# Scheduler priority for the ends, turned rows, routing and plan of a decoder's first expert layers

## The chip, the core and the metric

The kernel runs on one core of a Trainium2 chip. A core has five engines with instruction queues of their own: TensorE (PE in the profile, PEld for its weight loads), VectorE (DVE), ScalarE (ACT), GpSimd (POOL) and SyncE (SP), which here only starts DMA transfers. Each engine works through its queue in order; they wait for one another by semaphores. The metric is the device time of one execution in microseconds (us).

## What is computed

Two decoder layers over `x` of 16 batches of 128 rows by 256, everything in float32. Each sublayer's output is added to its input and normalised:

```
x = LN(x + causal attention, 16 heads of 64)            # layer 0
x = LN(x + sum_e gate_e * relu(x Win_e) Wout_e)         # 8 experts, gates from two inputs
x = LN(x + 2 shared experts + top-2 of 16 routed ones)
x = LN(x + banded attention, 16 heads of 16)            # layer 1
x = LN(x + cross attention on ctx)
x = LN(x + g/(g+1e-6) * sum_e (gelu(x w1_e + b1_e) w2_e + b2_e))   # 8 experts, all of them
```

The third line is the one that matters here. Router logits `x @ router_w` give a softmax; the best two of 16 experts and their weights are found for every row. The kernel collects the rows of each expert, so that each routed expert multiplies only its own rows.

## The kernel before, in words

**Groups and streams.** The 16 batches form 4 groups of 4 (512 rows). A piece of work is a Python generator that yields an estimated duration in us after each portion, or a condition, or a time until which it waits. A `Weaver` (lines 216 to 256) interleaves them while the program is written: a main stream (attention layers), a side stream `dense` (expert layers), and short streams, which are taken first whenever their time has come. `after` (1270) adds a short stream. `run` (1276) names the layers: (0, g) is attention, (1, g) the first expert layer of group g, (2, h) the routed experts of half h (groups 2h and 2h+1), (3, g) and (4, g) the attentions of layer 1, (5, g) the last experts. The dense stream does (1,0) (1,1) (2,0) (1,2) (1,3) (2,1) and then the four last expert layers; (2, h) is written only once the half's plan has been written (1279).

**From program order to queues.** The Tile framework makes the queue of each engine before launch. It steps through a simulated time: when an engine is free, it takes, of the instructions whose inputs are ready by its estimates, the one that ranks first, which is the one written first in the program. An instruction written later can go earlier if it is ready earlier. `tc.high_priority()` makes what is written inside it rank as if written at the program's start. Tiles with the same tag share a fixed number of buffers; they are handed out in the order in which the program asks. PSUM has two banks each of the tags H, M and O and one double bank S. Projections, hidden layers, turned rows, routing logits and the plan's counts all use H; expert products use M; attention uses S for scores and O for turned weights and products.

**The first expert layer** (`ensemble0`, 807, with `products`, 681). TensorE computes hidden layers (tag H) and, by a Strassen scheme, 7 block products per expert (tag M), which DVE adds up in `acc` (721). When the last expert is done, POOL and DVE combine the 7 sums into `y` (743 to 753), and `finish` adds a short stream: `products_end`, followed by `tail(1, g)`.

**`products_end`** (756) waits 2.5 us of written time. In two halves it turns `y` on TensorE (763), adds it to `x` and takes the statistics on DVE (290, 300, 301); `done` (303) computes the deviation's inverse on POOL (308) and normalises on DVE (310).

**`tail(1, g)`** (1243) waits, then `transposed` (261) turns the 4 normalised batches on TensorE (268); DVE copies the first turned half (270), ACT the second (272). `route` (840) follows: 8 matmuls for logits (845), and a chain of some 25 small DVE instructions and one on ACT (858 to 892) for the best two experts and their weights.

**`plan`** (928) follows the routing of the second group of a half. Two matmuls count the rows per expert (936), a chain of DVE instructions (942 to 987) computes where each row goes (`places`), and 16 indirect DMAs on POOL (992) scatter the rows of `x` to `copies` in HBM. `experts0` (1003) first does the two shared experts of both groups, then loads scattered rows (`load_rows`, 1063, which waits for all 16 scatters), turns them (`turn`, 1074) and does the 16 pairs of row tiles.

Of the kernel before, what the change touches and what calls it, by code (L numbers as in the profile page):

```python
# [29 lines left out]
def kernel(ctx: ExitStack, tc: tile.TileContext, a: dict, out: bass.AP):  # L30
# [15 lines left out]
    def bank(tag):  # L46
        return ps.tile([P, T], F32, tag=tag, name=f"ps{tag}")
# [7 lines left out]
    def transpose(out_, in_):  # L55
        n = in_.shape[0]
        return nc.tensor.transpose(out_, in_, ident[:n, :n])  # L57
# [36 lines left out]
    def load_up(name, *parts):  # L94
        return load_w("up", 1024, name, *parts, bufs=3)
# [114 lines left out]
    UNTIL = "until"  # L210

    class Stream:
        def __init__(self, gen):
            self.gen, self.at, self.can, self.share, self.over = gen, 0.0, None, 0.0, False

    class Weaver:

# [5 lines left out]
        def piece(self, t):  # L223

            t.can = None
            try:
                got = next(t.gen)
            except StopIteration:
                t.over = True
                return 0.0  # L230
            if callable(got):
                t.can = got
            elif isinstance(got, tuple):
                t.at = got[1]
            else:
                self.now += got
                return got
            return 0.0
# [19 lines left out]
    weaver = Weaver()  # L258


    def transposed(x, xT=None):

        if xT is None:
            xT = xp.tile([P, KC, T], F32, tag="xT", name="xT")
        for c in range(KC):
            pt = bank("H")
            for b in range(GB):
                transpose(pt[:, b * P:(b + 1) * P], x[:, b, c * P:(c + 1) * P])
            if c == 0:
                nc.vector.tensor_copy(xT[:, c, :], pt)  # L270
            else:
                last = nc.scalar.copy(xT[:, c, :], pt)
        return xT, last

    class Norm:
# [27 lines left out]
        def done(self, first=0, n=GB):  # L303
            at = slice(first, first + n)
            ve = sp.tile([P, GB], F32, tag="ve", name="ve")
            nc.vector.tensor_scalar(ve[:, at], self.mv[:, at, 1], EPS, None, ALU.add)  # L306
            rstd = sp.tile([P, GB], F32, tag="rstd", name="rstd")
            nc.gpsimd.tensor_tensor(rstd[:, at], ve[:, at], mhalf[:, at], ALU.pow)  # L308
            for b in range(first, first + n):
                nc.vector.tensor_scalar(  # L310
                    self.x[:, b, :], self.x[:, b, :],
                    self.mv[:, b, 0:1], rstd[:, b:b + 1], ALU.subtract, ALU.mult,
                )

    def project(pt, w, cols, xT):

        for c in range(KC):
            mm(pt, lhsT=w[:, c, cols], rhs=xT[:, c, :], start=c == 0, stop=c == KC - 1)
# [340 lines left out]
    def load_blocks(layer, e, g, w):  # L659

        if (layer, e) in in_hbm:
            got, = load_down("wb", in_hbm[layer, e])
            return got.rearrange("p s (q d) -> p s q d", q=2)

        raw, = load_w("up", 1024, "raw", w, bufs=3, later=True)
        raw = raw.rearrange("p (q l) (j d) -> p q l j d", l=2, j=2)
        b00, b01, b10, b11 = (raw[:, :, l, j, :] for l in range(2) for j in range(2))
        t = wp.tile([P, 7, 2 * P], F32, tag="down", name="wb0")
        blocks = t.rearrange("p s (q d) -> p s q d", q=2)
        minus = [(4, b01, b00), (5, b11, blocks[:, 4]), (2, blocks[:, 5], b10), (3, b11, b01)]  # L670
        for s, one, two in minus:
            step = nc.gpsimd.tensor_tensor(blocks[:, s], one, two, ALU.subtract)
            together(step, *transposed_by[g])
        for s, one in ((0, b00), (1, b10), (6, b11)):
            together(nc.gpsimd.tensor_copy(blocks[:, s], one), *transposed_by[g])
        held = dp.tile([P, 7, 2 * P], F32, tag=f"wb{layer}", name="wbd", bufs=8)
        nc.gpsimd.dma_start(out=held, in_=t)
        in_hbm[layer, e] = held
        return blocks
# [76 lines left out]
    def products_end(t, norm, scale, done):  # L756

        yield UNTIL, weaver.now + 2.5
        for i in (1, 0):
            pt = bank("H").rearrange("p (b d) -> p b d", b=2)  # L760
            for b in range(2):
                for j in range(2):
                    transpose(pt[:, b, j * P:(j + 1) * P], t[:, j, i, b * P:(b + 1) * P])
            for b in range(2):
                at = 2 * i + b
                norm.add(at, pt[:, b, :], None if scale is None else scale[:, at:at + 1])
            done(norm, 2 * i)
            yield 0.5
# [3 lines left out]
    def gates0(g):  # L772

        it = p2.tile([P, GB, P], I32, tag="it", name="it", bufs=1)
        nc.sync.dma_start(
            out=it, in_=a["itok_BxS2xS_0_7"][g * GB:(g + 1) * GB].rearrange("b k s -> k b s")
        )
        cx = load_ctx(g).rearrange("p b s -> p (b s)")
        held = dp.tile([8, T], F32, tag="gates", name="gatesd", bufs=NG)
        for q in range(2):  # L780
            chose = []
            for r in range(4):
                t = p4.tile([P, T], F32, tag="cw", name="chose")
                step = nc.vector.scalar_tensor_tensor(
                    out=t, in0=it.rearrange("p b s -> p (b s)"), scalar=float(4 * q + r), in1=cx,
                    op0=ALU.is_equal, op1=ALU.mult,
                )
                together(step, *transposed_by[g])
                chose.append(t)
            yield UNTIL, weaver.now + 3.5  # L790

            pg = bank("H")
            for r in range(4):
                mm(
                    pg[32 * r:32 * r + 32, :], lhsT=ones[:, :32], rhs=chose[r],
                    start=True, stop=True,
                )
            sums = p4.tile([P, T], F32, tag="cw", name="sums")
            nc.scalar.copy(sums, pg)
            for r in range(4):  # L800
                nc.sync.dma_start(
                    out=held[4 * q + r:4 * q + r + 1, :], in_=sums[32 * r:32 * r + 1, :]
                )
            yield 1.0
        gates_of[g] = held

    def ensemble0(x, xT, g):
        def load(e):
            gt = p2.tile([P, T], F32, tag="sg", name="gt")
            nc.sync.dma_start(out=gt, in_=gates_of[g][e:e + 1, :].to_broadcast([P, T]))  # L810
            return load_up(f"we0_{e}", a["L0_xattn_proj_in"][e])[0], gt

        def hidden(h, up, e, c):
            ph = bank("H")
            project(ph, up[0], slice(c * P, (c + 1) * P), xT)
            nc.vector.scalar_tensor_tensor(  # L816
                out=h, in0=ph, scalar=0.0, in1=up[1], op0=ALU.max, op1=ALU.mult
            )

        norm = Norm(x)  # L820
        yield from products(
            load, lambda e: load_blocks(0, e, g, a["L0_xattn_proj_out"][e]), hidden,
            lambda t: after(
                products_end(t, norm, None, lambda norm, b: norm.done(b, 2)), tail(1, g)
            ),
        )

# [175 lines left out]
    def experts0(half):  # L1003
# [153 lines left out]
        def collect():  # L1157
# [3 lines left out]
            for g in groups:  # L1161
# [15 lines left out]
                after(tail(2, g))  # L1177

        after(collect())

    def gate1(xT):
# [61 lines left out]
    def tail(number, g):  # L1243

        if number >= 0:
            yield UNTIL, weaver.now + 7.0
        xTs[g], last = transposed(xs[g], xTs[g])
        transposed_by[g] = [last]
        yield 0.9
        if number == 0:  # L1250
            yield from gates0(g)
        elif number in (1, 4):
            yield UNTIL, weaver.now + 2.5
            if number == 4:
                extra[g] = yield from gate1(xTs[g])
            else:
                yield from route(xTs[g], g)
                if written[g ^ 1] == 1:
                    yield from plan(g // 2)
        written[g] = number  # L1260
# [6 lines left out]
            out=out[at:at + 2].rearrange("b p d -> p b d"), in_=norm.x[:, b:b + 2, :]  # L1267
        )

    def after(*gens):  # L1270
        def both():
            for gen in gens:
                yield from gen
        weaver.short.append(Stream(both()))

    def run(number, g):

# [120 lines left out]
```

## Time and profile before

| | |
|---|---|
| median of 3 runs | 1773.87 us (1773.58 to 1775.16) |
| the profiled execution | 1788.15 us |
| its span, first to last instruction | 1786.5 us |
| TensorE granted clock, mean | 0.977 |
| TensorE busy | 1683.4 us, 94% |
| DVE, ACT, POOL busy | 1135.9, 658.8, 491.4 us |
| routing of groups 0 to 3, first DVE step (L858), first and last | 388.5 us, 1030.4 us |
| scatters of the first plan, of the second (L992), first start | 575.08 us, 1053.83 us |

In the profile a line such as L858 is a line of the kernel. A row of a timeline gives the start, the duration, engine, line, operation, output and inputs by the program's names, the shape and the count of merged instructions; in brackets stands how long the engine had been idle before it and what ended that wait. Matmuls of one group are listed as pairs of passes, since float32 takes two. A row of a stage gives its start and end, its length, then the busy time and number of instructions of PE, PEld, DVE, ACT and POOL, the granted TensorE clock (1.00 is full), the DMA share and GB/s. The "chain that ended last" follows the execution back from its last instruction: at each step to what released it.

### The profile page before, as it was taken

The numbers are of one execution on the slowest core, as the hardware profiler recorded it, in microseconds if no ns is written. First come the engines' busy times: TensorE is split into PE (matmuls) and PEld (weight loads), VectorE is DVE, ScalarE is ACT, GpSimd is POOL, SyncE is SP. The second block draws the span as 40 slices with busy tenths as digits, with TensorE's granted clock in tenths as the row PEclk, the third lists the DMA queues.
The fourth block names the chain that finished last, engine by engine and source line by source line (L and its number), as shares of the span: only waits on it lengthen the run. The fifth ranks groups of instructions, "written<-read, shape, count | busy, mean of one in ns | idle before, by whom it ended". The sixth has DMA issues, their size and how long they took to land.

```text
span 1786.5 us, 21794 instructions
## 1 busy us (share of the span) xinstructions
PE 1683.4 (94%) x7644; PEld 1043.0 (58%) x7644; DVE 1135.9 (64%) x2209; ACT 658.8 (37%) x1758; POOL 491.4 (28%) x492
## 2 busy tenths in 40 slices
PE   9999999999998899999999888979999999999996
PEld 6656556666665565555556455546555555556664
DVE  4565655576657336777886754685667766685544
ACT  4534311111124250034121434642955668373121
POOL 5311223210012304132321341473533133230000
PEclk9999999999999899999999988989999999999998
DMA  9321333433311396332313018533241211212331
GB/s 269 120 72 41 107 133 121 136 100 115 124 51 39 109 312 230 110 109 78 96 58 114 16 39 298 166 117 112 100 139 60 76 55 68 75 65 98 109 118 33
DMA packets 96702, 195.95 MB, mean 110 GB/s; under 512 B 15960, under 2 KB 58000, under 8 KB 96528
## 3 DMA queue, kind: packets, MB, share of 16 engines
q1 hardware_dynamic: 90688, 171.01, 28.8%
q0 software_dynamic: 5904, 23.54, 3.7%
q8 instruction: 61, 1.00, 0.3%
q14 instruction: 49, 0.40, 0.1%
HBM read 165.09 MB, written 37.81 MB: 114 GB/s over the span
## 4 chain that ended last, share of the span: by engine, by line
PE 71%; DVE 13%; issue 6%; ACT 5%; DMA 2%; POOL 2%; another core or an unknown queue 0%; POOLq 0%; DVEq 0%; ACTq 0%; SPq 0%
PE psH L52 40%; PE psM L52 19%; PE psO L57 3%; PE psS L52 3%; PE psO L52 3%; PE psH L57 2%; ACT e L369 2%; DVE nmax L354 1%; DVE x L310 1%; DMA wquad<-in_L_attn_W_Q 1%; DVE h L816 1%; DVE x L292 1%; POOL rstd L308 1%; DVE e L349 1%; DVE acc L721 1%
## 5 line engine op out<-in xcount | busy, mean ns | idle before, releaser
L52 PE MATMUL psH<-xT,we 128*128 128x512 f32 x1024 | 493.8, 604 | 8.3 <-ACT h L1226 4.9
L375 POOL TENSOR_TENSOR e<-e,inv 128x512 f32<-128x512 f32 (+1 forms) x128 | 190.3, 1487 | 501.2 <-DVE inv L374 446.5
L52 PEld LDWEIGHTS psH<-xT,we 128*128 128x128 f32 x1024 | 186.8, 191 | 173.9 <-issue 141.7
L369 ACT ACTIVATE e<-e,nmax 128x128 f32<-128x128 f32 x512 | 198.6, 389 | 196.6 <-DVE nmax L354 175.0
L52 PE MATMUL psM<-cm,wb 128*128 128x256 f32 x1024 | 265.1, 383 | 1.5 <-DVE acc L721 1.5
L52 PEld LDWEIGHTS psM<-cm,wb 128*128 128x128 f32 x1024 | 192.6, 191 | 70.6 <-issue 45.1
L721 DVE TENSOR_TENSOR acc<-psM,acc 128x512 f32<-128x512 f32 (+1 forms) x216 | 135.2, 626 | 123.5 <-PE psM L52 122.8
L52 PE MATMUL psM<-h,wb 128*128 128x256 f32 x768 | 200.7, 384 | 1.6 <-ACT h L1226 1.6
L384 ACT COPY eT<-psO 128x512 f32<-128x512 f32 x192 | 106.8, 584 | 232.9 <-PE psO L57 230.9
L52 PEld LDWEIGHTS psM<-h,wb 128*128 128x128 f32 x768 | 142.7, 190 | 65.1 <-issue 45.1
L1226 ACT ACTIVATE h<-psH,b 128x512 f32<-128x512 f32 x128 | 87.5, 688 | 188.5 <-PE psH L52 186.5
L816 DVE SCALAR_TENSOR_TENSOR h<-psH,gt 128x512 f32<-128x512 f32 x128 | 87.7, 686 | 80.9 <-PE psH L52 78.1
L57 PE MATMUL psO<-ident,e 128*128 128x128 f32 x768 | 118.3, 286 | 12.4 <-POOL e L375 8.5
L57 PEld LDWEIGHTS psO<-ident,e 128*128 128x128 f32 x768 | 90.7, 145 | 62.6 <-issue 37.7
L52 PE MATMUL psH<-xT,wquad 128*128 128x512 f32 x256 | 118.9, 608 | 3.4 <-DMA wquad<-in_L_attn_W_Q 3.1
L503 POOL TENSOR_TENSOR kb<-kT,hm 128x512 f32<-128x512 f32 x64 | 71.1, 1112 | 153.1 <-PE psS L52 99.1
L369 ACT ACTIVATION_READ_ACCUMULATOR e<-e,nmax 128x1 f32 x512 | 95.8, 187 | 0.0
L52 PE MATMUL psO<-eT,v 128*64 128x128 f32 (+1 forms) x1024 | 84.5, 346 | 6.2 <-ACT eT L384 5.4
L308 POOL TENSOR_TENSOR rstd<-ve,mhalf 128x4 f32<-128x4 f32 (+1 forms) x32 | 28.5, 890 | 211.8 <-DVE ve L306 211.7
L354 DVE TENSOR_REDUCE nmax<-e 128x4 f32<-128x512 f32 (+1 forms) x96 | 82.5, 859 | 1.9
L52 PE MATMUL psS<-kb,qT 64*128 64x512 f32 x256 | 74.2, 656 | 7.4 <-DVE e L349 3.0
L52 PEld LDWEIGHTS psH<-xT,wquad 128*128 128x128 f32 x256 | 47.2, 192 | 56.7 <-issue 47.4
(215 smaller groups left out, 2296.2 us busy)
## 6 DMA issues: line engine op xcount, KB each, us to landing
wb<-wbd SPq DMA_DIRECT2D x48, 896.0 KB
we<-in_L_xattn_proj_in SPq DMA_DIRECT2D x32, 512.0 KB
wt<-table SPq DMA_DIRECT2D x64, 256.0 KB
we<-in_L_ffn_w SPq DMA_DIRECT2D x32, 512.0 KB
wbd<-wb POOLq DMA_DIRECT2D x16, 896.0 KB
gt<-gatesd SPq DMA_DIRECT2D x32, 256.0 KB
results<-y SPq DMA_DIRECT2D x10, 768.0 KB
rows<-copies SPq DMA_DIRECT2D x6, 1024.0 KB
```

The source lines that it names most:

```text
L52: recent[0] = nc.tensor.matmul(*args, **how)
L57: return nc.tensor.transpose(out_, in_, ident[:n, :n])
L292: step = nc.vector.scalar_tensor_tensor(out=r, in0=y, scalar=scale, in1=r, op0=ALU.mult, op1=ALU.add)
L308: nc.gpsimd.tensor_tensor(rstd[:, at], ve[:, at], mhalf[:, at], ALU.pow)
L354: nc.vector.tensor_reduce(nmax.rearrange("p (s h) -> p s h", s=2), s, AX.X, ALU.max, negate=True)
L369: nc.scalar.activation(e[:, h, :], s[:, h // (n // 2), h % (n // 2), :], AF.Exp, bias=nmax[:, h:h + 1], accum_out=total[:, h:h + 1],)
L375: nc.gpsimd.tensor_tensor(e, e, inv.unsqueeze(2).to_broadcast([P, n, P]), ALU.mult)
L384: return eT, nc.scalar.copy(eT, pt)
L503: nc.gpsimd.tensor_tensor(kb, kT[:, c, at].unsqueeze(1).to_broadcast([P, 4, P]), hm4.unsqueeze(2).to_broadcast([P, 4, P]), ALU.mult,)
L721: nc.vector.tensor_tensor(to, pm[:, :len(slots), :], to, ALU.add)
L816: nc.vector.scalar_tensor_tensor(out=h, in0=ph, scalar=0.0, in1=up[1], op0=ALU.max, op1=ALU.mult)
L1226: nc.scalar.activation(h, ph, AF.Gelu, bias=b1[:, 4 * e + c:4 * e + c + 1])
```

## The change

A stream can carry a flag `early`. While a portion of such a stream is written, the program is inside `tc.high_priority()`. The short stream that follows each first expert layer, `products_end` and `tail(1, g)` with its routing and, for groups 1 and 3, the plan and its 16 scatters, is marked so. The other short streams, and the ends of the last expert layers (`store`), are not. What is computed, the instructions and the order in which the program writes them are the same.

```diff
     class Stream:
-        def __init__(self, gen):
+        def __init__(self, gen, early=False):
             self.gen, self.at, self.can, self.share, self.over = gen, 0.0, None, 0.0, False
+            self.early = early
...
             t.can = None
             try:
-                got = next(t.gen)
+                with tc.high_priority() if t.early else nullcontext():
+                    got = next(t.gen)
             except StopIteration:
...
             lambda t: after(
-                products_end(t, norm, None, lambda norm, b: norm.done(b, 2)), tail(1, g)
+                products_end(t, norm, None, lambda norm, b: norm.done(b, 2)), tail(1, g),
+                early=True,
             ),
...
-    def after(*gens):
+    def after(*gens, early=False):
         def both():
             for gen in gens:
                 yield from gen
-        weaver.short.append(Stream(both()))
+        weaver.short.append(Stream(both(), early))
```

## The prediction

> **What bounds the kernel now.** I read the page first, the utilisation by stage second, the chain of waits third, and the timeline around the two plans last. The page's first part:
>
> ```profile
> span 1786.5 us, 21794 instructions
> PE 1683.4 (94%) x7644; PEld 1043.0 (58%) x7644; DVE 1135.9 (64%) x2209; ACT 658.8 (37%) x1758; POOL 491.4 (28%) x492
> ```
>
> TensorE is busy 1683.4 of 1786.5 us, so 103 us of idle time are all that a new order can win, besides stretches at a reduced clock. The stages show where they lie (start and end in us, length, busy time of PE, PEld, DVE, ACT and POOL, granted clock, DMA share, GB/s):
>
> ```profile
> 380.00:400.00 20.00, 20.00 (x88) 13.18 (x87) 14.31 (x41) 3.65 (x12) 1.04 (x1) 1.00 0.29 92
> 575.00:604.00 29.00, 21.22 (x91) 13.40 (x91) 8.67 (x17) 5.11 (x19) 16.59 (x17) 0.80 0.42 145
> 950.00:1000.00 50.00, 49.37 (x191) 31.30 (x190) 33.49 (x65) 5.63 (x21) 7.04 (x7) 1.00 0.28 90
> 1003.00:1043.00 40.00, 28.92 (x133) 17.50 (x132) 30.70 (x71) 24.55 (x107) 18.86 (x15) 0.72 0.03 7
> 1071.00:1085.00 14.00, 6.20 (x31) 4.80 (x32) 3.14 (x10) 3.95 (x10) 2.27 (x3) 0.64 0.69 230
> ```
>
> Away from the plans TensorE is full (20.00 of 20, at clock 1.00, where group 0 is routed). Around a plan it is not: 7.8 us idle in 575 to 604, 11.1 in 1003 to 1043 at clock 0.72, 7.8 in 1071 to 1085 at 0.64. The second plan's path, from the timeline:
>
> ```profile
> 1022.77 1.09 PE L57 MATMUL psH<-ident,x 128*128 128x128 f32 x8
> 1024.58 0.64 DVE L270 COPY xT<-psH 128x512 f32<-128x512 f32 x1
> 1025.76 0.40 PE L52 MATMUL psH<-rw,xT 128*128 128x16 f32 x2
> 1026.61 0.56 ACT L272 COPY xT<-psH 128x512 f32<-128x512 f32 x1
> 1027.31 3.08 PE L52 MATMUL psH<-rw,xT 128*128 128x16 f32 x14
> 1030.43 0.23 DVE L858 TENSOR_REDUCE r_nm<-psH 128x4 f32<-128x64 f32 x1 [2.61 <-PE psH L52]
> ...
> 1053.83 1.07 POOL L992 DMA_INDIRECT copies<-x,r_places  x1 [3.81 <-DVE zT L541]
> 1072.92 0.96 POOL L992 DMA_INDIRECT copies<-x,r_places  x1 [0.30 <-issue]
> 1075.90 0.70 SPq L1068 DMA_DIRECT2D rows<-copies  x2
> 1078.39 0.90 PE L57 MATMUL psH<-ident,rows 128*128 128x128 f32 x3 [7.46 <-DMA rows<-copies]
> ```
>
> Turning, routing and planning take 1022.8 to 1053.5, the 16 scatters 1053.8 to 1073.9 back to back (0.96 plus 0.30 us each), and TensorE then waits 7.46 us for their rows. A microsecond saved on this path is one saved at 1078.39. The same path of the first plan runs from 537.5 to 575.08; there the rows are loaded at 597.10 but turned only at 626.95, behind the shared experts.
>
> **The change, part by part.** It removes and adds no instruction: 4 ends with their turned rows and routings, and 2 plans, keep all their work and only rank first when several instructions are ready for one engine. So I ask at each step which earlier-written instruction it now passes.
>
> DVE, routing and plan: nothing. In the first plan L354 (0.60 us) runs between L863 and L864, and L477 between L864 and L865. Those belong to attention units written later than the routing; they slip in while a step waits for its predecessor. Rank does not close such gaps. The 10.0 us of routing (1030.43 to 1040.45) and the 13.1 us from the plan's matmuls to its places (1053.53) stay, covered or not.
>
> POOL: the 32 scatters already run with no other POOL work among them (20.2 us for each 16, first to last end). SP issues nothing of the early pieces; its row loads wait for the scatters and move with them. Both are costed at the shift, no more.
>
> TensorE and PSUM: each early step takes its bank of tag H in turn, after the H tiles written before it, so it passes only work on banks S, O and M.
>
> First plan, three gains. The turn of the first y half, at 537.73, has its input from L751 at 536.23: up to 1.4 us, but the second half needs L753 (537.50), so I take half, 0.7. The turned x, ready at 546.19, is taken at 547.22 behind 8 records of values that began at 545.60: bound 1.0; the records already begun stay ahead, so 0.5. The routing matmuls start at 551.08 though the copy on ACT ends at 549.88, with transposes, an output and a product of attention between: bound 1.2, I take 1.1, since only a release is left. Sum 2.3, bounds 0 and 3.6. The attention passed here is late next; it has 7.8 us of idle TensorE after 575 to go into.
>
> Second plan. The turned x is done at 1023.86, but ACT copies it at 1026.61, after six exponentials begun from 1024.31 on, 0.385 us apart. Passing them brings the copy 2.3 us forward. TensorE cannot use it all: its scores run to 1025.83, and 16 routing records at this clock take 0.40 + 3.08 = 3.5 us, ending at 1029.3 instead of 1030.4. I take 1.2, between 0 and 2.4. Behind it come the passed exponentials, 0.56 us later each, and the four transposes of 1026.69; no dense work waits for them.
>
> The clock after that wait: it is granted at 0.64 on average from 1071 to 1085, so full speed returns late. If rows come 1.2 us earlier, some slow time may go. Were all the 6.20 busy us there at half speed, 3.1 would be slowness: the upper end; 0 is the lower. I take 0.6, a fifth of it, as the shift is a fifth of the 6.20. The Trainium skill, page "TensorE: Matmul & The Clock Gate", Part 1, speaks against counting on it: the gate looks at fixed windows of about 3.4 us, so an arrival inside the same window buys nothing. By that rule the term would be either 0 or a whole window's half, and this total 0.6 worse or 1.1 better; no row here fixes the window's phase after the shift.
>
> Second plan's sum 1.8, bounds 0 and 5.5.
>
> Losses, at the same steps in all four groups. In group 0 the second turn ends near 385.07, ACT's copy runs 385.10 to 385.69, and 1.89 us of products on bank M, 384.90 to 386.6, cover it before the routing matmuls. If these rank before the products, TensorE stands still for up to 0.7 us until the copy is there, in a stage where it has none to spare. The order is made beforehand by estimated times, so it would only happen where the estimate is early. I take two such places at 0.4, 0.8 us in all; the lower end is 0, the upper 20 places (two turns of y, two of x, one routing in each of 4 groups) at 0.7, 14 us. I stand near the lower end because the waits for turned x found now are small: nothing at group 0.
>
> Sum: 2.3 + 1.8 - 0.8 = 3.3 us less. The profiled execution took 1788.15 us (span 1786.5 and 1.65 around it) and would take 1784.85. The median of the three runs, 1773.87, lies 14.28 below it; I carry the difference over: **1770.6 us**. A change of 0.2%, about what a measurement of this kernel can tell from none, is 3.55 us; the forecast lies just inside it.
>
> **Rivals.**
>
> *Cover lost (slower).* Place: the twenty TensorE steps above, worst where it is full, at 380 to 400 and 950 to 1000. TensorE works in order, so a turn or routing matmul put before products that are ready makes those wait too, and DVE's sums and the next hidden layers behind them. Price 0.7 us each; the gains of 4.1 are eaten at six places, and 0.2% slower is reached at eleven. Twelve give 1773.87 - 4.1 + 8.4 = 1778.2. For it: before has waits of up to 2.8 us on DVE x L290 and 1.8 on r_one L876. Against: the order is made from estimated readiness, and the present one already lets the early steps through soon.
>
> *Nothing.* The early steps hold low places already, because the weaver prefers short streams; the bank order keeps the rest. Then 1773.9, give or take 1. For it: DVE and POOL show no overtaking at all. Against: ACT's 2.75 us from turn to copy at 1023.86.
>
> *More goes.* At 591.5 to 597.9 the chain has 6.39 us of "another core or an unknown queue": DVE L349 and, behind it, TensorE (7.78 us) stand until the first scatters have landed. If a changed order lets that work fall before the scatters' end, these go too: 3.3 + 6.4 = 9.7 less, 1764.2. Against: nothing in the change touches the scatters.
>
> **How the numbers follow.** Forecast 0.42 (own range 1766 to 1773, which reaches further down than up from 1770.6, so 0.24 faster by more than 3.55 us and 0.18 within), more goes 0.15 (faster), nothing 0.12 (within), cover lost 0.31 (0.28 slower, 0.03 within). So faster 0.39, within 0.33, slower 0.28. The range, 1763 to 1780, runs from the third rival to past the first, and leaves out the far end of the twenty places.
>
> **What would show it.** Right: routing of group 3 begins 1 to 2 us sooner after its y (now 18.7 us from L753 at 1011.73 to L858 at 1030.43); L272 follows its turn within 1 us; the 16 scatters still take 20 us; the wait for rows falls below 6.5 us. The 10 us of routing on DVE should be unchanged; if they shrink, my reading of rank there is wrong and the gain is larger. New waits of TensorE for xT, y or x near 385 and 965 would show the cover lost. Wrong also if the two plans' stages keep their times and the difference arises elsewhere, from an order that shifted after them.

## The result and the profile after

The changed kernel takes 1778.53 us (1776.08 to 1783.96), the kernel before on the same chip 1774.51 (1771.65 to 1775.84). The ratio on record is 1.0033, 95% interval 1.0022 to 1.0043: slower by 0.33%, where 0.2% faster was forecast. (The recorded ratios are formed from the runs; the quotient of the two medians alone is 1.0023.) Repeated on two other chips, where the kernel before takes 1785 to 1786 us, the ratio was 1.0005 (0.9994 to 1.0017) and 1.0009 (0.9997 to 1.0020). So the change gains nothing that can be measured anywhere, and costs between nothing and 0.4%. Every ratio below is to the kernel before on the same chip.

The page of the profile after, its first part (line numbers are now 2 or 3 higher than before):

```profile
span 1779.4 us, 21776 instructions
PE 1676.9 (94%) x7644; PEld 1037.8 (58%) x7644; DVE 1140.3 (64%) x2209; ACT 659.4 (37%) x1758; POOL 491.6 (28%) x492
```

Taken alone this page says the opposite of the runs: its span is 7 us below that of the profile before. That profile happened to lie 14 us above the median of its kernel, this one 2.5 us above. A change of some 4 us is not to be read from two spans. I read it from stretches that repeat from profile to profile.

The stages that answer to those shown before, the last three put at the same distance from the work around the second plan (start and end, length, busy time of PE, PEld, DVE, ACT, POOL, clock, DMA share, GB/s):

```profile
380.00:400.00 20.00, 19.85 (x92) 12.34 (x91) 16.18 (x41) 4.14 (x18) 2.08 (x2) 1.00 0.28 92
575.00:604.00 29.00, 25.71 (x109) 15.21 (x108) 12.56 (x27) 6.22 (x21) 17.59 (x18) 1.00 0.40 132
939.00:989.00 50.00, 49.37 (x190) 31.31 (x188) 33.60 (x65) 5.63 (x21) 7.16 (x7) 1.00 0.27 90
992.00:1032.00 40.00, 26.72 (x122) 15.45 (x121) 30.71 (x66) 22.71 (x97) 16.74 (x14) 0.67 0.03 7
1064.60:1078.60 14.00, 6.50 (x36) 4.73 (x36) 2.63 (x9) 2.21 (x5) 4.21 (x4) 0.55 0.67 230
```

Group 0's routing loses a little TensorE time (19.85 of 20). At the first plan TensorE is busy 25.71 of 29 instead of 21.22; a second profile of the changed kernel has only 21.53 of 29 at the same place, so this gain is a chance of one execution (more on it below). The full stretch ahead of group 3's ends is untouched (49.37 both times). At the second plan 2.2 us of TensorE's work are missing from the 40.

The second plan's path after, from the timeline:

```profile
1010.17 1.97 PE L57 MATMUL psH<-ident,x 128*128 128x128 f32 x8 [1.13 <-DVE x L312]
1015.88 1.96 PE L52 MATMUL psH<-rw,xT 128*128 128x16 f32 x16
1017.88 0.23 DVE L861 TENSOR_REDUCE r_nm<-psH 128x4 f32<-128x64 f32 x1 [0.65 <-PE psH L52]
1019.55 1.90 POOL L377 TENSOR_TENSOR e<-e,inv 128x1024 f32<-128x1024 f32 x1 [2.40 <-DVE inv L376]
1020.47 1.06 DVE L868 TENSOR_TENSOR r_p<-r_p,r_t 128x64 f32<-128x64 f32 x1
1026.38 3.76 POOL L377 TENSOR_TENSOR e<-e,inv 128x1024 f32<-128x1024 f32 x2 [4.93 <-DVE inv L376]
1026.55 1.81 DVE L876 TENSOR_TENSOR r_at<-r_at,order 128x64 f32<-128x64 f32 x1
1028.29 1.88 DVE L890 TENSOR_SCALAR r_den<-r_den 128x4 f32<-128x4 f32 x1
1030.60 1.22 PE L52 MATMUL psH<-r_one,before 128*128 128x256 f32 x2 [2.66 <-DVE r_one L879]
1034.46 1.90 POOL L377 TENSOR_TENSOR e<-e,inv 128x1024 f32<-128x1024 f32 x1 [4.32 <-DVE inv L376]
1034.49 1.92 DVE L953 COPY r_work<-r_work 128x64 f32<-128x64 f32 x1
1047.47 1.07 POOL L995 DMA_INDIRECT copies<-x,r_places  x1 [11.11 <-DVE mv L303]
1071.99 0.90 PE L57 MATMUL psH<-ident,rows 128*128 128x128 f32 x3 [10.65 <-DMA rows<-copies]
```

And the kernel before, profiled a second time, at the same place:

```profile
1019.86 1.90 POOL L375 TENSOR_TENSOR e<-e,inv 128x1024 f32<-128x1024 f32 x1 [0.71 <-DVE inv L374]
1022.14 1.90 POOL L375 TENSOR_TENSOR e<-e,inv 128x1024 f32<-128x1024 f32 x1 [0.38 <-DVE inv L374]
1024.12 0.23 DVE L858 TENSOR_REDUCE r_nm<-psH 128x4 f32<-128x64 f32 x1 [1.18 <-PE psH L52]
1027.47 1.90 POOL L375 TENSOR_TENSOR e<-e,inv 128x1024 f32<-128x1024 f32 x1 [3.43 <-DVE inv L374]
1027.79 1.66 DVE L872 TENSOR_TENSOR r_at<-r_p,r_m 128x64 f32<-128x64 f32 x1
1031.16 0.23 DVE L873 TENSOR_TENSOR r_at<-r_at,order 128x64 f32<-128x64 f32 x1
1031.30 0.16 DVE L887 TENSOR_SCALAR r_den<-r_den 128x4 f32<-128x4 f32 x1
1037.12 0.19 DVE L950 COPY r_work<-r_work 128x64 f32<-128x64 f32 x1
1046.36 1.07 POOL L992 DMA_INDIRECT copies<-x,r_places  x1 [3.81 <-DVE zT L541]
1070.94 0.90 PE L57 MATMUL psH<-ident,rows 128*128 128x128 f32 x3 [7.47 <-DMA rows<-copies]
```

Here is one part of the loss. The same small DVE steps take 0.23, 0.16 and 0.19 us before and 1.81, 1.88 and 1.92 after. Each of the long ones begins just after a multiply on POOL and ends when that ends: 1026.55 + 1.81 = 1028.36 beside the first of the two at 1026.38, which ends at 1028.28, and 1034.49 + 1.92 = 1036.41 beside 1034.46 + 1.90. Before, two of those multiplies (1019.86, 1022.14) were over when the routing began at 1024.12. After, the routing begins at 1017.88 and three of four lie inside it. These are multiplies of attention units that have nothing to do with the plan. Why they had moved was the first question.

### What the change writes besides what it says

The answer is in the ranks of the instructions. `Weaver.piece` writes each portion with `next(t.gen)` inside `tc.high_priority()`. When a short stream is at its end, `next` raises `StopIteration`, and the exception leaves the block. The old rank is then not restored: the counter goes on from where the high-priority block had it, close to 0. This happens four times, once at the end of each group's stream; the counter falls to 0 from 1747, 768, 1197 and 667. In the kernel before it rises to 8104 without a break. So from each end on, everything written later ranks ahead of everything written earlier that still waits: attention, shared experts, all of it. I call this the restart. In the queues, 576 of TensorE's 4422 places differ from before and 412 of DVE's 2209; with the same pieces early but no restart it is 214 and 300.

### The profile page after: what moved, and what is told of

Read it like the earlier page. It is cut to its first block, busy times and chain, and to the rows that moved or that the text cites. A ratio compares the mean times of both kernels' runs of the same rounds, so it can differ in the third digit from the quotient of the medians.

```text
span 1779.4 us, 21776 instructions
## 1 busy us (share of the span) xinstructions
PE 1676.9 (94%) x7644; PEld 1037.8 (58%) x7644; DVE 1140.3 (64%) x2209; ACT 659.4 (37%) x1758; POOL 491.6 (28%) x492
## 4 chain that ended last, share of the span: by engine, by line
PE 72%; DVE 14%; ACT 5%; POOL 3%; DMA 2%; issue 2%; POOLq 0%; DVEq 0%; SPq 0%; ACTq 0%
PE psH L52 40%; PE psM L52 19%; PE psS L52 4%; PE psO L57 4%; PE psO L52 3%; PE psH L57 2%; ACT e L371 2%; DVE nmax L356 2%; DVE x L312 1%; DVE e L351 1%; POOL rstd L310 1%; POOL copies L995 1%; DVE h L818 1%; DVE x L294 1%; DVE acc L723 1%
## 5 line engine op out<-in xcount | busy, mean ns | idle before, releaser
L52 PEld LDWEIGHTS psM<-h,wb 128*128 128x128 f32 x768 | 142.5, 190 | 67.4 <-issue 47.0
L57 PE MATMUL psO<-ident,e 128*128 128x128 f32 x768 | 117.9, 285 | 18.7 <-POOL e L377 16.5
L356 DVE TENSOR_REDUCE nmax<-e 128x4 f32<-128x512 f32 (+1 forms) x96 | 82.4, 859 | 1.9
```

Of the source, the lines that this page charges most:

```text
L52: recent[0] = nc.tensor.matmul(*args, **how)
L356: nc.vector.tensor_reduce(nmax.rearrange("p (s h) -> p s h", s=2), s, AX.X, ALU.max, negate=True)
```

## The experiments

The path lengths come from one profile in each case, measured from the start of the last step of `y` (L753 in the kernel before) to TensorE's first turn of scattered rows. The last column runs from the second plan's rows to the end of the span. The three profiles of the kernel before differ by 2.4 and 2.6 us on these paths, so a difference of that size in a single profile is not to be read alone.

| kernel | ratio to before (95%) | first plan, us | second plan, us | rows to end, us |
|---|---|---|---|---|
| before (three profiles) | 1 | 89.86, 87.47, 88.56 | 66.66, 64.09, 65.45 | 708.07, 707.93, 709.04 |
| after (three profiles) | 1.0033, 1.0005, 1.0009 | 76.93, 85.55, 83.93 | 71.38, 71.29, 69.17 | 707.37, 707.37, 707.02 |
| early_clean | 1.0009 (0.9998, 1.0019) | 87.15 | 65.48 | 709.49 |
| restart_only | 1.0078 (1.0059, 1.0096) | 84.94 | 74.16 | 710.82 |
| only_g1 | 0.9979 (0.9966, 0.9992) | 85.20 | 65.50 | 708.40 |
| r1_none | 0.9979 (0.9967, 0.9991) | 84.87 | 65.43 | 708.45 |
| only_g3 | 1.0025 (1.0012, 1.0037) | 90.81 | 71.42 | 707.53 |
| clean_g3 | 1.0007 (0.9994, 1.0020) | 87.48 | 65.55 | 709.88 |
| pool_out | 1.0001 (0.9988, 1.0014) | 84.68 | 67.71 | 710.03 |
| act_mult | 0.9971 (0.9961, 0.9982) | 85.13 | 67.39 | 703.73 |
| act_only | 1.0003 (0.9984, 1.0021) | 88.39 | 69.87 | 704.13 |
| act_both | 0.9959 (0.9941, 0.9977) | 86.10 | 69.86 | 704.09 |

### Priority alone, restart alone

early_clean keeps the early pieces and lets no exception leave the block. restart_only writes no piece early and restarts the counter at the four ends.

```diff
 early_clean
-            try:
-                with tc.high_priority() if t.early else nullcontext():
-                    got = next(t.gen)
-            except StopIteration:
+            with tc.high_priority() if t.early else nullcontext():
+                got = next(t.gen, "over")
+            if got == "over":
                 t.over = True
                 return 0.0
 restart_only
             try:
-                with tc.high_priority() if t.early else nullcontext():
-                    got = next(t.gen)
+                got = next(t.gen)
             except StopIteration:
                 t.over = True
+                if t.early:
+                    try:
+                        with tc.high_priority():
+                            raise KeyError
+                    except KeyError:
+                        pass
```

> The changed kernel with one thing mended: a stream that ends no longer leaves the high priority block by an exception, so that the rank of what is written later goes on from where it was instead of starting again from 0 (four times in the changed kernel, at the ends of the four short streams). Theory 'restart' (the loss comes from the rank that starts again, which puts later work ahead of earlier work): 1769 to 1773 us, ratio 0.997 to 0.999 to the kernel before, as forecast for the early pieces alone. Theory 'cover' (the early pieces themselves cost TensorE its cover): 1778 to 1779 us, ratio 1.002 to 1.003, as the changed kernel.

> The other half: no piece is written early, but at the end of each of the four short streams the rank starts again from 0, as in the changed kernel. Theory 'restart': 1777 to 1783 us, ratio 1.002 to 1.005; the routing and plan of group 3 are dealt out with other attention work between their steps. Theory 'cover': 1774 to 1775 us, ratio 0.999 to 1.001.

Measured: 1.0009 (0.9998 to 1.0019) and 1.0078 (1.0059 to 1.0096). What the change is named for does nothing that can be measured. What it does by the way costs 0.78% when it stands alone. Neither theory gave the first number: the early pieces alone neither win 0.1 to 0.3% nor lose 0.2 to 0.3%; and the restart alone costs more than its theory's 0.5%. Early pieces plus an explicit restart at the four ends give exactly the queues of the changed kernel, so no third part is left.

The stage at group 0 agrees. The same row of stages, of early_clean:

```profile
380.00:400.00 20.00, 20.00 (x89) 13.02 (x88) 15.11 (x40) 3.76 (x12) 1.04 (x1) 1.00 0.28 92
```

and of restart_only:

```profile
380.00:400.00 20.00, 19.52 (x127) 12.86 (x128) 14.62 (x31) 9.07 (x38) 4.77 (x5) 1.00 0.12 40
```

The small loss there belongs to the restart. At the second plan restart_only is worst, and TensorE's and ACT's timeline show by what:

```profile
1020.30 1.09 PE L57 MATMUL psH<-ident,x 128*128 128x128 f32 x8
1025.46 0.29 PE L52 MATMUL psH<-rw,xT 128*128 128x16 f32 x2
1032.34 0.56 ACT L279 COPY xT<-psH 128x512 f32<-128x512 f32 x1
1032.96 3.17 PE L52 MATMUL psH<-rw,xT 128*128 128x16 f32 x14 [3.26 <-ACT xT L279]
```

The turned rows are ready at 1021.39 and copied at 1032.34. In between ACT runs exponentials of attention units written later, which now rank first. The prediction had seen 2.75 us of this in the kernel before; here it is 10.95. The early mark protects the copy from it, which is why the changed kernel (17.25 us from `y` to routing in its second profile, against 26.61 here) is not as slow as restart_only.

### Which end

only_g1 and only_g3 do for one group what the change does for all four. clean_g3 has group 3's pieces early without the restart. r1_none has no early piece and one restart, at the end of group 1's stream. In these kernels no exception leaves the block; `restart` runs the lines that restart_only adds.

```diff
 only_g1
+                early=g == 1, restart=g == 1,
 only_g3
+                early=g == 3, restart=g == 3,
 clean_g3
+                early=g == 3,
 r1_none
+                early=False, restart=g == 1,
```

> The whole change (early pieces, and the rank that starts again where the stream ends) for group 1 alone, the first plan. Theory 'two opposite parts' (the first plan wins about 10 us, the second loses about 6, group 0 loses about 1): ratio 0.993 to 0.996, 77 us from y of group 1 to its first turned rows, and the kernel is faster than both. Theory 'the first plan's gain is the chance of one execution' (a stall of VectorE and TensorE of 5 to 8 us in the scatters that was missing there): ratio 0.998 to 1.000, 85 to 88 us.

> The whole change for group 3 alone, the second plan. Theory 'two opposite parts': ratio 1.003 to 1.005, 70 to 72 us from y of group 3 to its first turned rows. If the loss of the second plan comes from the restart at the end of group 2 instead, 64 to 66 us and ratio 0.999 to 1.001.

> Group 3's pieces early, and the rank not started again. Theory 'restart': the second plan loses only what the early pieces alone lost in the kernel with all pieces early, 64 to 66 us from y to turned rows, ratio 0.999 to 1.001. Theory 'the early pieces of group 3 do it': 70 to 72 us, ratio 1.003 to 1.005.

> No piece early; the rank starts again from 0 at the end of group 1's stream alone. Theory 'the first plan's gain comes from the restart' (later work, the shared experts above all, goes ahead of attention that is left over): 84 to 86 us from y of group 1 to its turned rows, as with both parts (85.2), ratio 0.997 to 0.999. Theory 'it comes from the early pieces': 87 to 91 us as before, ratio 0.999 to 1.001.

The two plans pull in opposite directions. The restart after group 1 wins 0.21%, with or without early pieces; the first plan's path is 85 us instead of 88, as r1_none's first theory had it. The 77 us and the ratio of 0.993 to 0.996 that I had expected of only_g1 were wrong: they rested on the one profile of 76.93 us. The restart after group 3 costs: only_g3 less clean_g3 is 1790.90 - 1787.07 = 3.8 us, though the two intervals (1.0012 to 1.0037, 0.9994 to 1.0020) overlap a little. In the trace it is 71.42 - 65.55 = 5.9 us of path, of which 2.3 come back later (707.53 against 709.88).

I split the 5.9 into its steps. The first 1.9 us lie ahead of the routing. In both kernels ACT has copied the turned rows 12.2 us after the start of `y`'s last step. But in only_g3 TensorE takes a product first, and the scores that stand before the routing matmuls in both run at a granted clock of 0.50 there, of 0.96 in clean_g3 (ACT and TensorE, only_g3, then clean_g3):

```profile
1021.86 0.59 ACT L279 COPY xT<-psH 128x512 f32<-128x512 f32 x1 [1.30 <-PE psH L57]
1022.61 1.08 PE L52 MATMUL psO<-eT,v 128*32 128x256 f32 x8
1023.62 2.08 PE L52 MATMUL psS<-kb,qT 64*128 64x512 f32 x4
1025.63 1.97 PE L52 MATMUL psH<-rw,xT 128*128 128x16 f32 x16
1022.00 0.59 ACT L273 COPY xT<-psH 128x512 f32<-128x512 f32 x1 [2.87 <-PE psH L57]
1022.74 1.15 PE L52 MATMUL psS<-kb,qT 64*128 64x512 f32 x4
1023.83 1.96 PE L52 MATMUL psH<-rw,xT 128*128 128x16 f32 x16
```

Order and clock cost about 1 us each. The clock is not the order's alone: the third profile after has the order of only_g3 there but a clock of 1.00 at these scores, and its routing begins 16.0 us after `y` instead of 17.3. Another 1.6 us lie in the routing and 2.3 in the plan. Routing (from the first L858 to the second `r_one`, L876) takes 8.9 to 9.8 us before, 10.8 in clean_g3, 12.4 in only_g3 and after. The chain's own steps sum to about 3.8 us in each. Their lengthening beside POOL is 1.5 us before, 3.15 in clean_g3, 4.27 after. The plan (to `places`, L987) takes 13.1, 12.9 and 14.4 us in the three profiles before, 14.4 in clean_g3, 16.7 in only_g3, and 16.6, 16.6 and 15.6 after. There the lengthening hardly changes (1.8 to 1.9 us), but 11 steps of other work (6.8 us) run between its steps, where there are 7 (4.5 us) in clean_g3 and 6 (3.8 us) before: sums of the shared experts, and attention steps that an older rank had kept elsewhere. So against the kernel before, where routing and plan together are 5 to 7 us shorter, about 2.8 us are DVE steps held by POOL and about 2.9 are other work in the gaps. Against clean_g3 it is 1.1 and 1.9 of 4.0; the rest is waiting.

That the early pieces alone do not help, though they do what I had hoped at ACT, is seen in clean_g3 and early_clean: from `y` to routing 15.4 us instead of 17.3, then 10.8 instead of 8.9 to 9.8 for routing and 14.4 for the plan, where before had 12.9, 13.1 and 14.4. The gain is gone when the scatters begin.

### The changed kernel again

> The changed kernel once more, on the same chip and beside the same runs of the kernel before as the three that follow. Ratio 1.002 to 1.004 again. In its profile: 76 to 78 us from L755 of group 1 (the last step of its y) to its first turned rows, 70 to 72 us for the same of group 3 (87.5 and 64.1 in the second profile of the kernel before).

Measured 1.0005 (0.9994 to 1.0017), with 85.55 us at the first plan and 71.29 at the second: the ratio and the first path were missed, the second path came. A third set gave 1.0009 (0.9997 to 1.0020), for which and for the two further profiles of before I had written:

> The changed kernel beside it. Without late signals the first plan has nothing to win: 76 to 78 us there, and the second plan's loss of about 6 less some clock remains, ratio 1.002 to 1.004. With late signals 84 to 86 us at the first plan, ratio 0.9995 to 1.0015.

> The kernel before, unchanged, for a second profile. Its eight times lie between 1771.65 and 1775.84 us, its first profiled execution took 1788.15. If the stall of TensorE at 590.9 to 598.67 us (7.78 us) belongs to the kernel, it is found again and the execution takes about 1788; if it was a chance of that one execution, the stall is under 4 us, and the execution takes 1772 to 1778.

> The kernel before on another chip. In its two profiles so far the completion signals of TensorE and VectorE come late by up to 14 us while POOL issues the 16 scatters (21 and 19 of some 45 of TensorE's are over 0.7 us late); in the first profile of the changed kernel none of 49 is. If that is a condition of chip or execution and not of the kernel, an execution of the kernel before without late signals takes 1772 to 1776 us and goes from y of group 1 to its turned rows in 77 to 80 us; one with them takes 1780 to 1790, and 87 to 91.

The stall of before came again (5.95 us, though that execution took 1780.55 us and not 1788) and a third time (7.9 us). The terms taken from the two later pairs of profiles add up to this. First plan: mean 84.7 against 88.0, -3.3. Second plan 70.2 against 64.8, +5.5. From group 0's `y` to group 1's it takes 168.6 us instead of 167.5, +1.2. After the second plan 1.3 come back. Together +2.1, or 0.12%, inside both later intervals but below the first chip's. What is more on that chip stays open: its two profiles, of which one lay 14 us above its median, cannot tell.

The profiles also differ in one thing that no order explains. In the kernel before, TensorE stands still behind a DVE step whose releaser is given as remote:

```profile
595.14 0.69 DVE L349 TENSOR_TENSOR e<-psS,causal 128x512 f32<-128x512 f32 x1 [5.72 <-remote]
595.88 1.22 PE L52 MATMUL psS<-kT,qT 64*128 64x128 f32 x8 [5.95 <-DVE e L349]
```

In the first profile after, the stall of this place was 3.29 us long:

```profile
597.64 0.33 PE L57 MATMUL psO<-ident,e 128*128 128x128 f32 x1 [3.29 <-POOL e L377]
```

That seemed to be the rival "more goes" come true, and the 76.93 us of that profile rest on it. In the second it was 4.07 + 3.40 us, in the third 6.72, with the same queues. One step shows the difference. The second profile before and the first after have the same scores on TensorE at nearly the same time; only in the latter does DVE take them up at once (before, then after):

```profile
587.58 0.72 PE L52 MATMUL psS<-kT,qT 64*128 64x128 f32 x8
587.59 0.71 PE L52 MATMUL psS<-kT,qT 64*128 64x128 f32 x8
588.42 0.69 DVE L351 TENSOR_TENSOR e<-psS,causal 128x512 f32<-128x512 f32 x1
```

In the former DVE starts on them at 595.14, the row above. The reason shows in the semaphores. While POOL issues the 16 scatters, many of TensorE's completion signals are recorded more than 0.7 us after the instruction's end, up to 8 us: over both plans 13 of 25 in the profile before, 15 of 25 and 14 of 25 in its repeats, 12 of 24 in the second and in the third after; in the first profile after 0 of 29. Outside the scatters it is at most 13 of some 1520. (These traces also hold 9 to 14 fewer records of that semaphore than instructions that raise it, the first after none fewer. So some of the late ones may be lost records; the stalls themselves are not.) So I read this stall as late news, not order, and one execution escaped it. What delays the signals I could not find, and no kernel was tried that takes the scatters away.

### Is it POOL's multiplies?

pool_out is the changed kernel without three multiplies, of the units that fall into group 3's routing: their attention weights are not divided by their sums. The act kernels do the same multiplies on ACT, one call for each head: act_mult those of five units around the second plan in only_g1, act_only the same five in the kernel before, act_both these and six around the first plan in r1_none.

```diff
 pool_out
-        nc.gpsimd.tensor_tensor(e, e, inv.unsqueeze(2).to_broadcast([P, n, P]), ALU.mult)
+        seen_units.append(n)
+        if len(seen_units) - 1 not in (83, 84, 85):
+            nc.gpsimd.tensor_tensor(e, e, inv.unsqueeze(2).to_broadcast([P, n, P]), ALU.mult)
 act_mult, act_only; act_both with units 54 to 59 as well
+        if len(seen_units) - 1 in (83, 84, 85, 86, 87):
+            for h in range(n):
+                nc.scalar.activation(e[:, h, :], e[:, h, :], AF.Copy, scale=inv[:, h:h + 1])
+        else:
+            nc.gpsimd.tensor_tensor(e, e, inv.unsqueeze(2).to_broadcast([P, n, P]), ALU.mult)
```

> The changed kernel without the three multiplications on POOL (L377, 1.9 us each) that run during the routing of group 3: the weights of three attention units are not divided by their sums. In the changed kernel these steps of VectorE (L861 to L879, second) take 12.44 us, 4.27 of them stretched beyond the duration that the same steps have elsewhere. Theory 'POOL holds VectorE' (a step of VectorE that reads SBUF alone stands while POOL multiplies): the stretch falls below 0.5 us, the steps take 8 to 9 us, and from y of group 3 to its turned rows 67 to 68 us instead of 71.3. Theory 'the stretched steps wait for something else, POOL only runs beside them': stretch 3 to 4.5 us, 12 to 12.5, and 71 us.

> The whole change for group 1 alone, and the multiplications by inv of the five attention units around the second plan on ACT (8 of 128x128 each) instead of POOL. Nothing is left out. Theory 'POOL holds VectorE': the steps of routing and plan of group 3 lose their 3.3 us of stretch, y of group 3 to its turned rows 61 to 63 us instead of 65.5, ratio to the kernel before 0.995 to 0.997. If ACT becomes the bound there (it is busy 27 of 44 us, and gets about 14 more), 66 to 70 us and ratio 0.998 to 1.001.

> The kernel before with one thing changed: the multiplications by inv of the five attention units around the second plan on ACT instead of POOL; no rank is touched. If they are worth as much without the change of group 1, the ratio is 0.998 to 0.9995, the routing steps of group 3 take 6.5 to 7.5 us (8.9 to 9.8 before), the first plan stays at 87 to 91 us from y to rows. If their gain needs the other order, the ratio is 0.9995 to 1.001.

> The rank started again at the end of group 1's stream alone, no piece early, and the multiplications by inv of six attention units around the first plan and of five around the second on ACT. If the two gains add, the ratio is 0.995 to 0.997, the first routing and plan lose their 2.9 us of stretch (17.3 us together instead of 20.2). If ACT holds the first plan up, as it held back the start of the second routing by 3.3 us, 0.997 to 0.999.

That POOL holds these DVE steps is confirmed. In pool_out POOL is free during the routing, and the two steps have their short times again (timeline of POOL and DVE):

```profile
1021.57 1.04 POOL L509 TENSOR_TENSOR kb<-kT,hm 128x512 f32<-128x512 f32 x1 [6.27 <-PE psS L52]
1031.14 0.22 DVE L880 TENSOR_TENSOR r_at<-r_at,order 128x64 f32<-128x64 f32 x1
1031.28 0.16 DVE L894 TENSOR_SCALAR r_den<-r_den 128x4 f32<-128x4 f32 x1
1040.35 1.90 POOL L381 TENSOR_TENSOR e<-e,inv 128x1024 f32<-128x1024 f32 x1 [17.74 <-DVE inv L378]
```

Routing takes 8.32 us instead of 12.44, and the path falls from 71.4, 71.3 and 69.2 in the three profiles after to 67.7. The time does not follow: 1.0001, and the last column shows why, since 2.7 us more pass after the rows (710.03 against 707.37). A microsecond on this path is not, as the prediction had it, a microsecond at the end. My reading, not tested, is that some attention that had gone ahead while the path was long is still to do.

On ACT the multiplies shorten the routing further (6.87 us), but the path ends later, not sooner. The routing begins 20.5 us after `y` instead of 17.3 in all three act kernels, and more is lost after the scatters (act_both, TensorE and ACT):

```profile
1069.85 1.07 ACT L398 COPY eT<-psO 128x512 f32<-128x512 f32 x2 [11.88 <-remote]
1070.49 1.08 PE L52 MATMUL psO<-eT,v 128*32 128x256 f32 x8 [9.54 <-ACT eT L398]
1076.63 0.49 PE L57 MATMUL psH<-ident,rows 128*128 128x128 f32 x3
```

ACT hears late, during the scatters, that its input is ready, and TensorE stands behind it for 9.54 us, so the rows are turned 10.5 us after the last scatter's start instead of 5.4, and act_mult missed its 61 to 63 us with 67.4. What follows is 4 us shorter. The 14 us after the rows are granted a clock of 1.00 in the act kernels, against 0.71 to 0.77 in the three profiles before; that may be most of the 4 us, but was not tested. In act_both the steps of the first plan lose their lengthening too (0.4 us instead of 2.6 in r1_none), yet routing and plan there take 21.0 us against 20.2 in r1_none, not the 17.3 of the expectation: other waits took its place. Alone in the kernel before the change to ACT is worth nothing (1.0003); with the restart after group 1, act_both takes 1780.62 us against 1784.01 for the kernel before, ratio 0.9959 (0.9941 to 0.9977; the two medians alone give 0.9981). It is faster than both kernels. How much of that is the restart's 0.21%, and whether the multiplies add to it, is not settled, as the intervals of r1_none (0.9967 to 0.9991), act_mult and act_both overlap.

## Why the prediction was wrong

**"It removes and adds no instruction ... and only rank first."** This is the step that failed. The instructions are the same, but the early pieces are not the only ones that change rank. At four places all later work moves ahead of all older work. I had read `with tc.high_priority()` around `next` and not asked what happens to the block when the generator ends. The code that shows it was in the diff. The runs show the step's price: with the block left normally the change costs 0.09% (-0.02 to 0.19%), and the restart alone 0.78%.

**First plan, -2.3.** It is nearer in size (-3.3 in two pairs of profiles) than in cause. The three places I had named won nothing: from `y` to routing 15.97 us against 15.99. With early pieces alone the plan's chain is 10.16 us instead of 11.4 and 11.55 in two of before's profiles, but 10.28 in the third; what is left comes from the restart after group 1, which alone gives 84.87 us.

**Second plan, -1.2.** ACT's copy does pass the exponentials, and early_clean's routing begins 1.9 us sooner than in before's two later profiles, within my bound of 2.4; in the changed kernel the restart puts attention on TensorE ahead of the routing and takes it back (17.3 us in two profiles, 16.0 in the third). "DVE, routing and plan: nothing" was wrong: rank decides which attention steps lie in the gaps of the routing and when POOL's multiplies fall. My text had named a shrinking of the 10 us as the sign of a wrong reading; they grew to 12.4, the plan from 12.9 to 14.4 us to 15.6 to 16.6. "POOL costed at the shift, no more" missed that POOL's other work holds DVE. In all +5.5 stands where -1.2 stood.

**Clock, -0.6.** The rows came later after `y`, not sooner, so the term had no gain to follow. The clock of the 14 us around the rows is 0.55 to 0.56 in the three profiles after, against 0.63 to 0.69 before. The wait just before the rows, 10.65 us in the first profile after, is 3.3 and 3.4 in the others, where other stalls take its place; my sign "below 6.5" says nothing here. The clock of one profile had misled me elsewhere too: the 14 routing records of 3.08 us, and so the 18.7 us from `y` to routing, came from a clock of 0.50; in the two repeats they run at 1.00 and take 1.74 us, and it is 17.3 us.

**Losses, +0.8.** Near in size, 1.2 us at group 0, and not for my reason. With early pieces alone TensorE is busy 20.00 of 20 there, and the full stretch ahead of group 3 is 49.37 in both kernels. The rival "cover lost" gave 1778.2 and the result is 1778.53, but the waits it counted on are not there: TensorE waits 4.1 us for `y` at six places, in the kernel before 4.0 us at five. The close number was luck.

**Scatters unchanged.** Right: 19.5 to 19.8 us from the start of `places` to that of the last scatter in every kernel.

**"A microsecond saved on this path is one saved."** Only in part: only_g3 loses 5.9 on the path and 3.8 in all against clean_g3, pool_out wins 1.5 to 3.7 on it and next to nothing in all.

## What to carry to other kernels

When a change puts a context around a generator or any call that can raise, follow the exception too: what stays changed after it may be larger than what was meant. A scheduler's rank is relative, so raising one piece decides which foreign work falls into its gaps and which engine runs beside it; ask for a chain of small DVE steps what POOL does meanwhile. And with a change of a few us, compare stretches between fixed events over several profiles before believing one span, or one stall that is gone.

## What the runs showed of the hardware

- A DVE step with its operands in SBUF stood until a POOL multiply that had begun earlier was over: 0.23 to 1.81 us, 0.16 to 1.88, a copy 0.19 to 1.92. Reductions and steps that read PSUM kept their times (the reduction L354, L356 after, takes 1.21 us either way; the 29 additions `x<-psH,x` that began beside such a multiply, in the first profiles before and after, took 0.39 to 0.43 us, elsewhere 0.42). From each step's time less its shortest, I estimate 50 to 60 us of this beside all of POOL's arithmetic in the kernel before, and about 5 more after. The Trainium skill, page "SBUF — State Buffer", section "Who interferes with whom", says that DVE and GpSimd share one pair of ports by an exclusive lock, that DVE needs it with two inputs from SBUF or in copies and scalar operations of the two-port mode, and never in a `tensor_reduce`; whoever issues first holds it for the whole instruction. These rows agree wherever they bear on it; that POOL waits for DVE in turn they do not show. The prediction had not asked it.
- Completion signals of TensorE are recorded up to 9 us late while POOL issues indirect scatters, 36 to 60% of them by more than 0.7 us in 15 of the 16 profiles; the stalls that follow reach 11.88 us (ACT in act_both). The same section says that PE and ACT never wait on anyone. That is said of ports; for an engine that waits for their signals the rows here show several us, with a cause that is open.
